# The end of a graph-and-attention kernel put in an order by hand: norms, transposes and bias adds between the products

## The chip, the cores and the metric

The kernel runs on 1 core of one Trainium2 chip. The metric is the device time of one execution in microseconds (us). A core has a matrix engine (PE; the loading of its stationary operand is listed apart as PEld), a vector engine (DVE), an activation engine (ACT), a general engine (POOL), an engine that here only issues transfers (SP), and 16 DMA engines that serve the transfers of all queues. Each engine works through its own instructions in order and waits for others by semaphores. Products are summed in PSUM; tiles lie in SBUF; HBM is the memory outside.

## The reference

A graph convolution with a residual, and then a transformer layer on 1250 nodes of width D = 1024, with 16 heads that gate 8 experts each. The change touches only the last sums and the feed forward:

```python
x = x + gnn(layernorm(x), edges, W, b)            # x1 in the kernel
src = layernorm(x)                                # z in the kernel
src2 = moe_attn(src, Wq, Wk, Wv, Wo, Wsel_v, Wsel_o)
#   ... last step of it: einsum('bhsp,bhse,hepd->bsd', o, go, Wo)
src = src + src2
src = ln(src, ln1_g, ln1_b)
src2 = relu(src @ W1 + b1) @ W2 + b2              # W1: 1024 x 512, W2: 512 x 1024
src = src + src2
out = x + ln(src, ln2_g, ln2_b)
```

`ln` subtracts the mean, divides by the root of the variance plus 1e-5, multiplies by a gain and adds a shift. All is float32.

## The kernel before

Nodes lie in NT = 10 tiles of KT = 125 rows; two tiles make a chunk of 250 columns (NQ = 5 chunks). Every float32 product is made as three products of a value's rounded part and its remainder: `dot` (L152 to L156) issues hi x hi, hi x lo, lo x hi. A weight block of 128 x 1024 is loaded by SP into `w_raw` (L127, a pool of 2), ACT rounds it into `w_hi` (L138) and DVE makes `w_lo` (L144); `move` (L147 to L150) is a transfer of 125 rows in two pieces of 112 and 13, by default on SP's queue.

**Outputs** (`outputs`). Its 16 blocks of 4 weights (`order`, `blocks`) run over the 5 chunks: 80 steps. A step (k, c) is, for i in 0, 1 (tile t = 2c + i) and for each half of the 1024 columns, a sum of 12 matmuls of 512 columns: four quarters. At its start the step loads the next block's weight number c (for c < 4) and asks for `gb`, the gates of the step after next (L928). After each quarter DVE adds the sum to `acc[t]` (L1018). After quarter (0, 0) DVE gates the next step's heads (`gated`, L949 to L951) and SP loads `oc` and `r` for the step after (L937, L943; `r` in two more pieces at chunk 4). After (0, 1) and (1, 1) ACT and DVE split what comes next into `go_hi` (L958) and `go_lo` (L960). After (1, 0) the weight loaded in this step is split. `acc`, one array in the profile, appears there under the names of the memory that it takes over: `acc`, `zT`, `gate_v`. The sums have 5 PSUM banks, the transposes 2 (`banks[:] = [5, 2]`).

**Feed forward** (`feed_forward`). For each chunk c: 4 sums over W1 of 24 matmuls of 256 columns (f in 0..3), each followed by relu on ACT (L1072), its rounding (L1073) and remainder (L1074) into `hT`; then 4 sums over W2 of 12 matmuls of 512 columns, added to `acc` (L1085). `first_norm(c)` norms the chunk's two tiles: `moments` on DVE (two L162, L164, a root on ACT L166, L168), `affine` on DVE (L178, L179), then `transposed` (L181 to L191): per half, four transposes on PE, a rounding on ACT, a remainder on DVE, into the two parts of `sT`; POOL adds `b2` to the tile (L1044). `last_norm(t)` loads `x1` (L150) from HBM, POOL adds the shift `c2` to it (L1053), and DVE does moments and affine with `x1` as the shift; SP stores the result.

**Order.** The program up to block 14 of the outputs stands under `tc.manual_schedule`: every engine, SP included, gets its instructions in the order in which the code issues them. Block 15 and the feed forward stand outside: there a planner orders each engine's instructions when the program is built. The tables of the feed forward and the first two tiles of `x1` came to stand where the attention ends, at 1978 us.

```python
    with tc.manual_schedule(engines=all_engines):
        for _ in range(4 * (NT * (2 * NP - 1) + 4) - made):
            next(main)
    next(tail)
    for _ in main:
        pass
    for _ in tail:
        pass
```

Of the kernel before, what the change touches and what calls it, by code (L numbers as in the profile page):

```python
# [11 lines left out]
F32 = mybir.dt.float32  # L12
F32R = mybir.dt.float32r
# [4 lines left out]
ALU = mybir.AluOpType  # L18
# [14 lines left out]
P = 128  # L33
# [39 lines left out]
def gnn_ffn_kernel(  # L73
# [50 lines left out]
    def loaded(block, raw=None):  # L124
        if raw is None:
            raw = raws[0].tile([P, D], F32, name="w_raw")
        nc.sync.dma_start(raw, block)  # L127
        return raw
# [47 lines left out]
    def affine(out, x, mean, rs, scale, shift):  # L176

        nc.vector.scalar_tensor_tensor(out, x, mean, scale, op0=ALU.subtract, op1=ALU.mult)  # L178
        nc.vector.scalar_tensor_tensor(out, out, rs, shift, op0=ALU.mult, op1=ALU.add)  # L179

    def transposed(targets, y, psum_tile):  # L181

        for half in range(2):
            p = psum_tile([P, 4, KT])
            for k in range(4):
                d0 = (4 * half + k) * P
                nc.tensor.transpose(p[:, k, :], y[:, d0 : d0 + P], ident[:KT, :KT])
            for hi, lo, c0, cols in targets:
                to = (slice(None), slice(4 * half, 4 * half + 4), slice(c0, c0 + cols.stop - cols.start))
                nc.scalar.copy(hi[to], p[:, :, cols])  # L190
                nc.vector.tensor_tensor(lo[to], p[:, :, cols], hi[to].bitcast(F32), ALU.subtract)  # L191
# [722 lines left out]

    acc = []

    def outputs(acc_pool, pool):

        last = QW * (NC - 1)

# [42 lines left out]
        order = [(j, half_e) for j in range(NP) for half_e in range(2)]  # L963
        blocks = {k: [wo[j, 4 * half_e + i] for i in range(4)] for k, (j, half_e) in enumerate(order)}
        steps = [(k, c) for k in range(len(order)) for c in range(NQ)]

        def acc_load(t):
            acc.append(acc_pool(t))
# [32 lines left out]
            yield  # L1001
        after = []
        for m, (k, c) in enumerate(steps):
            raw = loaded(blocks[k + 1][c]) if c < 4 and k + 1 < len(order) else None
            following = m + 1 < len(steps)
            fetch(m + 2, True)
            for i in range(2):
                t = 2 * c + i
                if k == 0 and t + 2 < NT:
                    acc_load(t + 2)  # L1010
                for half in range(2):
                    cols = slice(512 * half, 512 * half + 512)
# [5 lines left out]
                    nc.vector.tensor_tensor(acc[t][:, cols], acc[t][:, cols], p, ALU.add)  # L1018
                    if following and half:
                        parts[i] = parts_of(current, i)  # L1020
                    elif following and i == 0:
                        current = gated(found.pop(0), *held)
                        fetch(m + 2, False)
                    elif raw is not None:
                        after.append(rounded(raw))
                    yield
            if c == NQ - 1:
                w, after = after, []


    def feed_forward(ftab, work):
        b1_s = ftab.tile([P, NF], F32, name="b1_s")
        nc.sync.dma_start(b1_s, b1)
        g1, c1 = broadcast_row(ftab, ln1_g, "g1"), broadcast_row(ftab, ln1_b, "c1")
        b2_s = broadcast_row(ftab, b2, "b2_s")
        g2, c2 = broadcast_row(ftab, ln2_g, "g2"), broadcast_row(ftab, ln2_b, "c2")

        def first_norm(c):
            sT = [work.tile([P, ND, QW], F32R, name=f"sT{k}") for k in range(2)]
            for i in range(2):  # L1040
                s = acc[2 * c + i]
                affine(s, s, *moments(s, "a"), g1[:KT], c1[:KT])
                transposed([(*sT, KT * i, slice(0, KT))], s, side_bank)
                nc.gpsimd.tensor_tensor(s, s, b2_s[:KT], ALU.add)  # L1044
            for part in sT:
                nc.scalar.copy(part[:, :, 2 * KT :], part[:, :, : QW - 2 * KT].bitcast(F32))
            return sT

        def last_norm(t):
            s = acc[t]  # L1050
            x1 = work.tile([KT, D], F32, name="x1")
            move(x1, x1_d[t])
            nc.gpsimd.tensor_tensor(x1, x1, c2[:KT], ALU.add)  # L1053
            mean, rs = moments(s, "b")
            step = D if t < NT - 1 else D // 2
            for c in range(0, D, step):
                affine(s[:, c : c + step], s[:, c : c + step], mean, rs, g2[:KT, c : c + step], x1[:, c : c + step])
                move(out[KT * t : KT * (t + 1), c : c + step], s[:, c : c + step])

        sT = first_norm(0)  # L1060
        yield
        w1s = [weights(w1[k]) for k in range(4)]
        w2s = [weights(w2[k]) for k in range(4)]
        for c in range(NQ):
            hT = [work.tile([P, NF, QW], F32R, name=f"hT{k}", bufs=1) for k in range(2)]
            for f in range(NF):
                p = bank([P, QW])
                for d in range(ND):
                    w = [part[:, 512 * (d % 2) + P * f : 512 * (d % 2) + P * (f + 1)] for part in w1s[d // 2]]
                    dot(p, w, [part[:, d, :] for part in sT], d == 0, d == ND - 1)  # L1070
# [4 lines left out]
            if c + 1 < NQ:  # L1075
                sT = first_norm(c + 1)
            for i in range(2):
                s = acc[2 * c + i]
                for half in range(2):
                    cols = slice(512 * half, 512 * half + 512)  # L1080
                    p = bank([KT, 512])
                    for f in range(NF):
                        dot(p, [part[:, f, KT * i : KT * (i + 1)] for part in hT],
                            [part[:, cols] for part in w2s[f]], f == 0, f == NF - 1)
                    nc.vector.tensor_tensor(s[:, cols], s[:, cols], p, ALU.add)  # L1085
                last_norm(2 * c + i)

    f_ctx = ctx.enter_context(ExitStack())
    per_head = 4 * NT
    main, spare = [], []  # L1090

    def acc_tile(t):

# [10 lines left out]
    with tc.tile_pool(name="attp", bufs=1) as apool:  # L1104
        w = [weights(wv[0, k]) for k in range(4)]
        with tc.manual_schedule(engines=all_engines):
            heads = attention(apool)
            with tc.tile_pool(name="vpool", bufs=2) as vpool:
                for k, _ in enumerate(values(apool, vpool, w)):
                    if k >= per_head - lead:  # L1110
                        next(heads)
                    if k == H * per_head - 4 * NZ - 1:
                        z2_ctx.close()
                        ring[:0] = [ctx.enter_context(tc.tile_pool(name="ring2", bufs=3, side="right"))] * 3
                        gop = ctx.enter_context(tc.tile_pool(name="gop", bufs=1, side="right"))
                        main.append(outputs(acc_tile, gop))
                    elif main:
                        next(main[0])
            made = sum(1 for _ in zip(heads, main[0]))
# [6 lines left out]
    tail = feed_forward(ftab, work)  # L1126
# [82 lines left out]
```

## Time and profile before

| | us |
|---|---|
| median of 3 runs | 2961.8 (2959.9 to 2963.07) |
| the profiled execution | 2961.16 |
| its span, first to last instruction | 2959.4 |
| PE busy | 2849.7 (96%) |
| DVE busy | 2120.9 (72%) |
| ACT busy | 993.0 (34%) |
| POOL busy | 569.1 (19%) |

All figures below are from that one execution, and times are counted from the start of the span. A row of the timeline has the start, the duration, engine, line, operation, result and operands with their shapes, how many it merges, and in brackets how long the engine stood idle before and what released it. A row such as `x2` merges several instructions that follow each other; SP's rows are issues of transfers, not the transfers. Matmuls overlap in the pipeline, so their rows are longer than the distance between their starts. The granted clock of PE is 1.00 at full speed.

### The profile page before, as it was taken

Reading aid. Unit: us, or ns where it says so; the run is one execution under the profiler, and the core shown is the slowest. Engines: PE = TensorE matmul, PEld = TensorE weight load, DVE = VectorE, ACT = ScalarE, POOL = GpSimd, SP = SyncE. Lnnn points to the kernel's source line nnn. Section 1 sums busy time; section 2 is a strip of 40 time slices with the busy share of each in tenths; the row PEclk is TensorE's granted clock in tenths of the full one; section 3 lists DMA queues with packets and bytes.
Section 4 is the critical chain, followed back from the end, with each engine's and each line's share of the span. In section 5 each row is a group of like instructions: output and inputs, shape, how many; then the busy total and the mean of one; then the engine's idle time right before and its main releaser. Section 6 shows DMA issues by size and latency. Waiting matters only on the chain. (4 is left out here: it accounts for less than half of the span.)

```text
span 2959.4 us, 40398 instructions
## 1 busy us (share of the span) xinstructions
PE 2849.7 (96%) x14018; PEld 2349.2 (79%) x14018; DVE 2120.9 (72%) x3588; ACT 993.0 (34%) x1706; POOL 569.1 (19%) x945
## 2 busy tenths in 40 slices
PE   6989899999999999999999999899999999999998
PEld 4767699978887887788888888777777777777787
DVE  7974487647777777778778787866666666656885
ACT  5772233324343433434434344321111111111222
POOL 2000011113333333333333333310000000000113
PEclk9999899999999999999999999999999999999999
DMA  3114456644555554555555555884444444444312
GB/s 117 56 44 146 150 163 169 197 99 125 151 132 134 134 142 124 144 140 147 130 152 139 144 132 129 209 217 128 114 119 121 114 123 117 115 121 119 112 52 88
DMA packets 229320, 385.45 MB, mean 130 GB/s; under 512 B 43369, under 2 KB 176489, under 8 KB 228946
## 3 DMA queue, kind: packets, MB, share of 16 engines
q1 hardware_dynamic: 176898, 273.49, 33.3%
q0 software_dynamic: 51888, 104.18, 14.6%
q10 hardware_dynamic: 320, 5.12, 0.6%
q8 instruction: 111, 1.82, 0.3%
q14 instruction: 103, 0.84, 0.1%
HBM read 220.73 MB, written 62.16 MB: 96 GB/s over the span
## 5 line engine op out<-in xcount | busy, mean ns | idle before, releaser
L154 PE MATMUL mm<-w_hi,go_hi 128*125 128x512 f32 x1280 | 507.9, 397 | 4.5 <-DVE zT L1018 3.4
L155 PE MATMUL mm<-w_lo,zT 128*128 128x512 f32 (+1 forms) x1280 | 506.4, 396 | 4.3 <-DVE w_lo L144 3.9
L155 PE MATMUL mm<-w_lo,go_hi 128*125 128x512 f32 x1280 | 508.8, 398 | 0.0
L154 PE MATMUL mm<-w_hi,zT 128*128 128x512 f32 (+1 forms) x1280 | 506.5, 396 | 1.0 <-ACT w_hi L138 1.0
L156 PE MATMUL mm<-w_hi,go_lo 128*125 128x512 f32 x1280 | 506.7, 397 | 0.7 <-DVE go_lo L960 0.7
L156 PE MATMUL mm<-w_hi,zT 128*128 128x512 f32 (+1 forms) x1280 | 505.3, 395 | 0.0
L755 ACT CAST att_hi<-turned 128x512 fp32r<-128x512 f32 x400 | 239.5, 621 | 455.5 <-DVE turned L798 279.5
L736 POOL DMA_DIRECT2D turned<-p x640 | 342.5, 542 | 80.8 <-ACT p L725 44.3
L1018 DVE TENSOR_TENSOR zT<-zT,mm 125x512 f32<-125x512 f32 x256 | 175.5, 686 | 220.5 <-PE mm L156 216.3
L798 DVE STREAM_TRANSPOSE turned<-turned 128x1280 f32<-128x1280 f32 x160 | 232.4, 1490 | 135.7 <-DMA q<-kq_d 57.5
L958 ACT CAST go_hi<-gb 128x500 fp32r<-128x500 f32 x160 | 98.3, 615 | 660.1 <-PE mm L155 289.1
L724 DVE TENSOR_REDUCE most<-side 128x1 f32<-128x1250 f32 x160 | 231.0, 1444 | 108.2 <-PE side L721 106.7
L725 ACT ACTIVATE p<-side,most 128x1250 f32<-128x1250 f32 x160 | 209.2, 1307 | 289.4 <-DVE most L724 284.7
L154 PEld LDWEIGHTS mm<-w_hi,go_hi 128*125 128x125 f32 x1280 | 239.1, 187 | 66.0 <-DVE zT L1018 4.1
L156 PEld LDWEIGHTS mm<-w_hi,go_lo 128*125 128x125 f32 x1280 | 238.9, 187 | 61.9 <-DVE go_lo L960 1.2
L155 PEld LDWEIGHTS mm<-w_lo,go_hi 128*125 128x125 f32 x1280 | 238.7, 186 | 59.2
L156 PEld LDWEIGHTS mm<-w_hi,zT 128*128 128x128 f32 (+1 forms) x1280 | 238.0, 186 | 59.5
L155 PEld LDWEIGHTS mm<-w_lo,zT 128*128 128x128 f32 (+1 forms) x1280 | 238.4, 186 | 44.3 <-DVE w_lo L144 9.4
L154 PEld LDWEIGHTS mm<-w_hi,zT 128*128 128x128 f32 (+1 forms) x1280 | 238.3, 186 | 35.8 <-ACT w_hi L138 1.2
L760 DVE TENSOR_TENSOR att_lo<-turned,att_hi 128x512 fp32r<-128x512 f32 x400 | 262.4, 682 | 0.0
L778 PE MATMUL po<-att_hi,v 128*128 128x256 f32 (+1 forms) x800 | 215.0, 290 | 33.8 <-ACT o L785 33.5
L144 DVE TENSOR_TENSOR w_lo<-w_raw,w_hi 128x1024 fp32r<-128x1024 f32 x154 | 189.5, 1231 | 43.6 <-ACT w_hi L138 43.3
(234 smaller groups left out, 4611.3 us busy)
## 6 DMA issues: line engine op xcount, KB each, us to landing
turned<-p SPq DMA_DIRECT2D x640, 80.0 KB
turned<-p POOLq DMA_DIRECT2D x640, 80.0 KB, 3.3
gb<-g_d SPq DMA_DIRECT2D x160, 250.0 KB
w_raw<-in_wv SPq DMA_DIRECT2D x64, 512.0 KB
w_raw<-in_wo SPq DMA_DIRECT2D x64, 512.0 KB
q<-kq_d POOLq DMA_DIRECT2D x80, 256.0 KB, 4.3
oc<-o_d SPq DMA_DIRECT2D x160, 125.0 KB
kq_d<-qk_hi SPq DMA_DIRECT2D x64, 156.2 KB
```

Source lines behind the costliest of these rows:

```text
L144: (lo_engine or nc.vector).tensor_tensor(lo, raw, hi.bitcast(F32), ALU.subtract)
L154: nc.tensor.matmul(p, lhsT=lhs[0], rhs=rhs[0], start=start, stop=False)
L155: nc.tensor.matmul(p, lhsT=lhs[0], rhs=rhs[1], start=False, stop=False)
L156: nc.tensor.matmul(p, lhsT=lhs[1], rhs=rhs[0], start=False, stop=stop)
L724: nc.vector.tensor_reduce(most, side[:, :N], AX.X, ALU.max, negate=True)
L725: nc.scalar.activation(p[:, (2 * n + i) % 3, :N], side[:, :N], AF.Exp, bias=most, accum_out=inverse[h][:, 2 * c + i : 2 * c + i + 1])
L736: queue.dma_start(t[NB * a : NB * (a + 1), :, KA * b : KA * (b + 1)], both[NB * b : NB * (b + 1), :, KA * a : KA * (a + 1)])
L755: nc.scalar.copy(hi, x)
L760: nc.vector.tensor_tensor(lo, x, hi.bitcast(F32), ALU.subtract)
L778: nc.tensor.matmul(po, lhsT=v_of[h][:rows, t, :], rhs=part[:rows, :, NB * b : NB * (b + 1)], start=(first and b == 0 and part is parts[0]) ...
L798: nc.vector.transpose(turned[n][:, i], turned[n][:, i])
L1018: nc.vector.tensor_tensor(acc[t][:, cols], acc[t][:, cols], p, ALU.add)
```

## The change

Block 15 and the feed forward come under the manual order too, and a table `also` says what the outputs do after which quarter, on top of their own work. `at(k, q, ...)` enters it after quarter q (0 to 19) of block k; `end` is 15.

- Block 12: one of the five tables of 128 x 1024 is loaded after the first quarter of each step.
- Blocks 13 and 14: in each step one tile of `x1` is loaded after quarter (0, 0), DVE adds `c2` to it after (1, 0), and SP stores it to the same place in HBM. `last_norm` then loads the sum; POOL's adds are gone.
- Block 14 also loads and splits two of the W2 weights, into memory of their own; block 15 has W1 as its next block, and loads the other two of W2 at its end.
- Block 15: moments and affine of tiles 0 to 3, and the transposes of tiles 0 and 1 by halves, after quarters of their own.
- Feed forward: norms stand between the products of W1, transposes between those of W2, half by half; `b2` is added by DVE; the second norm of the odd tiles moves into the next chunk's products of W1. `sT` has one buffer instead of two.

```diff
-    def transposed(targets, y, psum_tile):
-
-        for half in range(2):
+    def transposed(targets, y, psum_tile, halves=(0, 1)):
+
+        for half in halves:
...
+        blocks[len(order)] = [w1[k] for k in range(4)]
...
-            raw = loaded(blocks[k + 1][c]) if c < 4 and k + 1 < len(order) else None
+            raw = loaded(blocks[k + 1][c]) if c < 4 else None
...
+                    for what, *args in also.pop((k, t, half), ()):
+                        what(*args)
                     yield
             if c == NQ - 1:
                 w, after = after, []
+        w1s.extend(w)
...
+        def w2_split(k):
+            parts = None
+            if k < 2:
+                parts = [ftab.tile([P, D], F32R, name=f"w2_{part}{k}") for part in ("hi", "lo")]
+                nc.scalar.copy(parts[0], w2s[k])
+            w2s[k] = rounded(w2s[k], None, parts)
+
+        def x1_load(t):
+            x1s[t] = work.tile([KT, D], F32, name="x1")
+            move(x1s[t], x1_d[t])
+
+        def x1_shift(t):
+            nc.vector.tensor_tensor(x1s[t], x1s[t], rows["c2"][:KT], ALU.add)
+            move(x1_d[t], x1s[t])
...
+        def turn(t, half):
+            c, i = divmod(t, 2)
+            if i == half == 0:
+                sTs[c] = [work.tile([P, ND, QW], F32R, name=f"sT{k}", bufs=1) for k in range(2)]
+            sT = sTs[c]
+            transposed([(*sT, KT * i, slice(0, KT))], acc[t], side_bank, (half,))
+            if half and c:
+                add_b2(t)
+            if i and half:
+                for part in sT:
+                    nc.scalar.copy(part[:, :, 2 * KT :], part[:, :, : QW - 2 * KT].bitcast(F32))
...
+        def last_affine(t, c, n):
+            cols = slice(c, c + n)
+            affine(acc[t][:, cols], acc[t][:, cols], *rss[t], rows["g2"][:KT, cols], x1s[t][:, cols])
+            move(out[KT * t : KT * (t + 1), cols], acc[t][:, cols])
+
+        def last_moments(t):
+            x1_load(t)
+            rss[t] = moments(acc[t], "b")
...
+        for q, (row, name) in enumerate(((ln2_b, "c2"), (ln1_g, "g1"), (ln1_b, "c1"), (b2, "b2"), (ln2_g, "g2"))):
+            at(end - 3, 4 * q, constant, row, name)
+        for t in range(NT):
+            k, q = divmod(4 * t, 2 * NT)
+            at(end - 2 + k, q, x1_load, t)
+            at(end - 2 + k, q + 2, x1_shift, t)
+        for k in range(2):
+            at(end - 1, 3 + 4 * k, w2_load, k)
+            at(end - 1, 5 + 4 * k, w2_split, k)
+            at(end, 15 + k, w2_load, 2 + k)
+        for t, q in enumerate((2, 5, 8, 12)):
+            at(end, q, first_moments, t)
+            at(end, q + 1, first_affine, t)
+        for k, q in enumerate((7, 10, 11, 14)):
+            at(end, q, turn, k // 2, k % 2)
         yield
...
+                t = (4, None, 5, 6, 7, 8, 9, None, None, None)[2 * c + f // 2]
+                if t is not None:
+                    (first_affine if f % 2 else first_moments)(t)
+                if c == 0 and f < 2:
+                    w2_split(2 + f)
+                elif c == 0:
+                    add_b2(f - 2)
+                if c and f == 2:
+                    last_moments(2 * c - 1)
+                if c and f == 3:
+                    last_affine(2 * c - 1, 0, D)
+            for k in range(4):
+                i, half = divmod(k, 2)
...
+                if k < 3 and c + 1 < NQ:
+                    for m in range(k, k + 1 + k // 2):
+                        turn(2 * (c + 1) + m // 2, m % 2)
+                if k == 1:
+                    last_moments(2 * c)
+                if k == 2:
+                    last_affine(2 * c, 0, D)
+        last_moments(NT - 1)
+        for c in range(0, D, D // 2):
+            last_affine(NT - 1, c, D // 2)
...
     with tc.manual_schedule(engines=all_engines):
-        for _ in range(4 * (NT * (2 * NP - 1) + 4) - made):
-            next(main)
-    next(tail)
-    for _ in main:
-        pass
-    for _ in tail:
-        pass
+        tail = feed_forward(ftab, work, also, w1s)
+        next(tail)
+        for _ in main:
+            pass
+        for _ in tail:
+            pass
```

`first_moments`, `first_affine`, `add_b2`, `w2_load` and `constant` are one call each: `moments(acc[t], "a")`, `affine` with g1 and c1, an add of `b2` on DVE, `loaded(w2[k])`, `broadcast_row`.

More of the change, by code (lines that the diff above doesn't have):

```diff
@@ L915, in gnn_ffn_kernel, with outputs @@
     acc = []
-    def outputs(acc_pool, pool):
+    def outputs(acc_pool, pool, also, w1s):
         last = QW * (NC - 1)
@@ L1028, in outputs, with feed_forward @@
                 w, after = after, []
-    def feed_forward(ftab, work):
+        w1s.extend(w)
+    def feed_forward(ftab, work, also, w1s):
         b1_s = ftab.tile([P, NF], F32, name="b1_s")
-        nc.sync.dma_start(b1_s, b1)
[L1034 to L1060, printed above, removed]
@@ new lines, in feed_forward, with constant, w2_load @@
+        rows = {}
+        w2s, x1s, sTs, rss = [None] * 4, {}, {}, {}
+        def constant(row, name):
+            rows[name] = broadcast_row(ftab, row, name)
+        def w2_load(k):
+            w2s[k] = loaded(w2[k])
+        def w2_split(k):
[7 more added lines that the diff above has]
+            move(x1s[t], x1_d[t])
@@ new lines, in x1_shift, with first_moments, first_affine @@
+        def x1_shift(t):
+            nc.vector.tensor_tensor(x1s[t], x1s[t], rows["c2"][:KT], ALU.add)
+            move(x1_d[t], x1s[t])
+        def first_moments(t):
+            rss[t] = moments(acc[t], "a")
+        def first_affine(t):
+            affine(acc[t], acc[t], *rss.pop(t), rows["g1"][:KT], rows["c1"][:KT])
+        def turn(t, half):
[9 more added lines that the diff above has]
+                    nc.scalar.copy(part[:, :, 2 * KT :], part[:, :, : QW - 2 * KT].bitcast(F32))
@@ new lines, in add_b2, with at @@
+        def add_b2(t):
+            nc.vector.tensor_tensor(acc[t], acc[t], rows["b2"][:KT], ALU.add)
+        def last_affine(t, c, n):
[5 more added lines that the diff above has]
+            rss[t] = moments(acc[t], "b")
+        def at(k, q, *what):
+            also.setdefault((k, q // 2, q % 2), []).append(what)
@@ new lines, in feed_forward @@
+        end = 2 * NP - 1
+        nc.sync.dma_start(b1_s, b1)
+        for q, (row, name) in enumerate(((ln2_b, "c2"), (ln1_g, "g1"), (ln1_b, "c1"), (b2, "b2"), (ln2_g, "g2"))):
[8 more added lines that the diff above has]
+            at(end, 15 + k, w2_load, 2 + k)
@@ L1061, in feed_forward @@
+        for t, q in enumerate((2, 5, 8, 12)):
[3 more added lines that the diff above has]
+            at(end, q, turn, k // 2, k % 2)
         yield
-        w1s = [weights(w1[k]) for k in range(4)]
-        w2s = [weights(w2[k]) for k in range(4)]
         for c in range(NQ):
@@ L1069, in feed_forward @@
                     w = [part[:, 512 * (d % 2) + P * f : 512 * (d % 2) + P * (f + 1)] for part in w1s[d // 2]]
-                    dot(p, w, [part[:, d, :] for part in sT], d == 0, d == ND - 1)
+                    dot(p, w, [part[:, d, :] for part in sTs[c]], d == 0, d == ND - 1)
                 r = work.tile([P, QW], F32, name="relu")
@@ L1074, in feed_forward @@
                 nc.vector.tensor_tensor(hT[1][:, f, :], r, hT[0][:, f, :].bitcast(F32), ALU.subtract)
-            if c + 1 < NQ:
-                sT = first_norm(c + 1)
-            for i in range(2):
-                s = acc[2 * c + i]
[L1079 to L1086, printed above, removed]
+                t = (4, None, 5, 6, 7, 8, 9, None, None, None)[2 * c + f // 2]
[11 more added lines that the diff above has]
+                i, half = divmod(k, 2)
+                s = acc[2 * c + i]
+                cols = slice(512 * half, 512 * half + 512)
+                p = bank([KT, 512])
+                for f in range(NF):
+                    dot(p, [part[:, f, KT * i : KT * (i + 1)] for part in hT],
+                        [part[:, cols] for part in w2s[f]], f == 0, f == NF - 1)
+                nc.vector.tensor_tensor(s[:, cols], s[:, cols], p, ALU.add)
+                if k < 3 and c + 1 < NQ:
[8 more added lines that the diff above has]
+            last_affine(NT - 1, c, D // 2)
     f_ctx = ctx.enter_context(ExitStack())
     per_head = 4 * NT
-    main, spare = [], []
+    main, spare, also, w1s = [], [], {}, []
     def acc_tile(t):
@@ L1115, in gnn_ffn_kernel @@
                         gop = ctx.enter_context(tc.tile_pool(name="gop", bufs=1, side="right"))
-                        main.append(outputs(acc_tile, gop))
+                        main.append(outputs(acc_tile, gop, also, w1s))
                     elif main:
                         next(main[0])
-            made = sum(1 for _ in zip(heads, main[0]))
+            for _ in zip(heads, main[0]):
+                pass
     main = main[0]
@@ L1125, in gnn_ffn_kernel @@
     work = f_ctx.enter_context(tc.tile_pool(name="fwork", bufs=2))
-    tail = feed_forward(ftab, work)
     with tc.manual_schedule(engines=all_engines):
-        for _ in range(4 * (NT * (2 * NP - 1) + 4) - made):
-            next(main)
-    next(tail)
-    for _ in main:
-        pass
-    for _ in tail:
-        pass
+        tail = feed_forward(ftab, work, also, w1s)
[3 more added lines that the diff above has]
+        for _ in tail:
+            pass
 def rotation():
```

## The prediction

> **What bounds the kernel now.** First the stretches of the end, by engine: after the two times come busy time (instructions) of PE, PEld, DVE, ACT, POOL, then granted TensorE clock, DMA share, GB/s.
>
> ```profile
> 2680.00:2740.00 60.00, 60.00 (x259) 47.73 (x258) 37.26 (x53) 10.56 (x15) 0.00 (x0) 1.00 0.44 122
> ...
> 2780.00:2800.00 20.00, 17.40 (x84) 13.77 (x82) 20.00 (x29) 5.52 (x12) 5.70 (x2) 1.00 0.24 64
> 2800.00:2820.00 20.00, 16.23 (x67) 12.47 (x68) 20.00 (x30) 4.20 (x10) 5.29 (x2) 0.86 0.00 1
> 2820.00:2840.00 20.00, 20.00 (x115) 17.59 (x114) 18.87 (x31) 5.39 (x10) 0.00 (x0) 0.89 0.17 53
> ...
> 2900.00:2920.00 20.00, 20.00 (x139) 18.35 (x139) 11.10 (x20) 5.49 (x14) 6.36 (x3) 1.00 0.34 104
> ```
>
> PE is full in the outputs and in the feed forward. It loses time only in the last output block, where DVE is 100% busy. The timeline of PE there has three waits:
>
> ```profile
> 2800.09 0.68 PE L187 MATMUL tr<-ident,zT 125*128 125x125 f32 x4 [2.69 <-DVE sT L191]
> ...
> 2813.86 0.50 PE L154 MATMUL mm<-w_hi,go_hi 128*125 128x512 f32 x1 [0.26 <-ACT go_hi L958]
> 2818.93 0.79 PE L154 MATMUL mm<-w_hi,go_hi 128*125 128x512 f32 x1 [3.42 <-DVE zT L1018]
> ```
>
> DVE is late there because norms of tiles that nobody needs yet stand before the outputs' own work, and because a DVE instruction lasts longer while POOL adds b2:
>
> ```profile
> 2794.24 3.42 DVE L179 SCALAR_TENSOR_TENSOR zT<-zT,rsa,c 125x1024 f32<-125x1024 f32 x1
> ...
> 2803.10 2.50 DVE L949 TENSOR_TENSOR oc<-oc 128x250 f32<-128x250 f32 x1
> ```
>
> L179 otherwise lasts 1.28, L949 0.41; POOL's adds run at 2793.30 (3.28) and 2802.88 (2.43).
>
> **What goes.** The waits: 2.69 + 0.26 + 3.42 = 6.4 us. After each long one matmuls start 0.43 us apart instead of 0.23, to 2803.9 and to 2824.4: 3.1 us hold 6 matmuls and 4 transposes (1.9 us at full clock), 5.5 us hold 13 matmuls (3.0), so 1.2 + 2.5 = 3.7 us. Sum 10.1. [...] Waits of up to 1.67 us (at 1945.0) left the clock at 1.00 in the trace. Further, the old schedule loads the tables and two x1 tiles in one lump at 1978 to 1992 and lets POOL add to x1 at 1997; PE then loses 0.7 us (1.26 busy of 2000 to 2002, a go_lo of 2.00 us). One table a step in block 12 waits for nothing and DVE is 62% busy: 0.7 gained. Total 10.8.
>
> **What comes, 1: x1 in blocks 13 and 14.** The largest new thing. Each of these ten steps now loads an x1 tile, adds c2 on DVE, and stores it again. SP's queue in a step of today:
>
> ```profile
> 2695.02 1.26 SPq L928 DMA_DIRECT2D gb<-g_d  x2
> 2699.23 1.23 SPq L937 DMA_DIRECT2D oc<-o_d  x2
> 2700.55 1.19 SPq L943 DMA_DIRECT2D r<-r_d  x2
> 2701.78 0.59 SPq L127 DMA_DIRECT2D w_raw<-in_wo  x1
> 2706.20 1.26 SPq L928 DMA_DIRECT2D gb<-g_d  x2
> ```
>
> A step is 11.2 us. Call 0 the step's first add (L1018 at 2696.50). oc goes out at 2.73, when gb (L951) is done; r 1.32 later; the x1 load takes the place of w_raw, at 5.28. The add of c2 stands behind the third quarter's add and w_lo: DVE comes to it at 5.6 + 0.6 + 1.1 = 7.35. The load has to land in 2.1 us. How long it takes, from SP's and POOL's rows of the feed forward:
>
> ```profile
> 2906.09 0.77 SPq L150 DMA_DIRECT2D out<-zT  x2
> 2906.96 1.35 SPq L150 DMA_DIRECT2D x<-x_d  x2
> ```
>
> ```profile
> 2912.45 2.40 POOL L1053 TENSOR_TENSOR x<-x,c 125x1024 f32<-125x1024 f32 x1 [13.21 <-DMA x<-x_d]
> ```
>
> 5.5 us behind a store of the same size; the other two such pairs give 6.0 and 6.2. In windows of 1 us the data of one transfer start some 1.25 us after the issue (w_raw: 2701.78, data from 2703), 500 KB fill 1.7 us of the engines, and the user starts 1.7 us after the last data. Alone it is thus 1.25 + 1.7/0.9 + 1.7 = 4.8 (bounds 4.4, as the store issued at 2881.92 had data after 0.85, and 6.2). So DVE stands still for 2.9 us in the first step. Behind it in DVE's queue are the last quarter's add, go_lo, and all of the next step; behind it on SP is the store, then w_raw and gb.
>
> It feeds itself. From the start of one c2 add: 1.13 + 0.6 + 0.6 (last quarter's add, go_lo, next step's add begins) + 2.73 + 1.32 + 1.23 = 7.6 to the next x1 load, + 4.8 to land = 12.4. By the transfers: 1.25 to the store's issue, 1.25 to its data, 8.2 of service a step (4.8 now, 0.43 of 11.2; a store and a load 3.4, summed over 2882 to 2891), 1.7 = 12.4 with engines full, 13.0 at 0.92. I take 12.7, 1.5 us over the step. Nine repeats: four at 1.5; two without a w_raw behind them, bound by the issues, 1.3 each; one with four r transfers instead of two (2.47 against 1.19), 2.6; the two behind w2 loads, by transfers (512 KB more, 1.6), 3.2 and 3.1. Together 6 + 2.6 + 2.6 + 6.3 = 17.5, with the first 2.9 = 20.4. What covers: go_lo of the last quarter is normally done at 9.75 and PE wants it at 13.76, so 4.0 are free. PE loses **16.3**. Bounds: 0 (landing in 3.3 or less closes the loop inside 11.2) and 23 (engines at 0.85: 13.8 a cycle). I take the middle, which both ways give. The stalls are 1.3 to 3 us each; where the clock falls PE uses time it would have waited. [...]
>
> The adds themselves, 1.2 us of DVE a step, lie in its idle 38%; that cover is gone where the wait takes it, which the loop counts.
>
> **What comes, 2: block 15 by hand.** DVE per step: four adds 0.6, gating 2.0, go_lo 2 x 0.6, w_lo 1.13 = 6.7 (starts apart). Added: four moments (0.6 + 0.6 + 0.12 and the round trip to ACT's root, 1.9), four affines 2.4, four halves of a turn 0.6, nearly all in quarters 2 to 14. Summed quarter by quarter, DVE's lag grows to 4.8 us at quarter 13; go_lo then misses PE by 0.7 us, once more by 0.3. Price **1.0** (0 to 5). Transposes wait for affines that are 3 quarters old: 0.
>
> **What comes, 3: feed forward.** Today 0 stalls. In the chunks c = 1 and 2 quarter f = 2 puts two moments (2 x 2.0) between hT of f = 2 and of f = 3, and ACT's relu of f = 3 stands behind both roots. relu then starts 2.9 us after the product, + 0.45 + 0.45 (copy) = 3.8; the first three f of the next product cover 9 x 0.231 = 2.1. Stall 1.5 to 1.7 per chunk. Where the second product's half is done, DVE has add, turn, b2 add (1.2, now its own), moments, then add, two turns, b2, affine (2.4): the last lo half of sT is ready 1.2 us after PE wants it in c = 1 and 2, 0.3 in c = 0 and 3. Sum 2 x 1.5 + 2 x 1.2 + 2 x 0.3 = **6.0** (2 to 9). Waits this short leave the clock. Taking POOL's sixteen adds off saves nothing on the path here, PE being full; they cost DVE ten b2 adds of 1.2, counted.
>
> **What comes, 4: the tail.** x1 of the last tile is today loaded at 2934; now its load stands behind the store of tile 8, which waits for its affine. With 0 the last matmul's end: add of quarter 2 at -2.6, affine 8 done at +0.5, store, load, landed 5.3 to 6.2 after the store's issue: +5.9 to 6.7. The last shift wants it at +3.8. Then two halves: done at 8.0 to 8.9, today 6.0; the last store's tail stays. **+2.2** (1 to 3).
>
> Sum against the profiled execution (2961.2 around a span of 2959.4; the median is 0.6 above): 2961.2 - 10.8 + 16.3 + 1.0 + 6.0 + 2.2 = 2975.9. Forecast **2976**.
>
> **Rivals.** (a) *The waits for x1 don't add up:* landing in some 3.3 us, the 4.0 of slack absorb what is left; term 1 is 0: 2959.6, within 0.2%. For it: w_raw's lone engine time is short; against: no row lands under 4.4. (b) *It does what it says, faster:* as (a), and DVE's queue in the feed forward clears earlier than I add it up (waits 1, tail 1, block 15 0): 2961.2 - 10.8 + 2 = 2952.4. For it: DVE is only 55% busy from 2900 to 2920. It decides if landing is under 3.3 and roots return within a quarter. (c) *The one SP queue fills:* engines at 0.85, cycle 13.8, term 1 = 23, and half clock after waits over 2.7 us adds 3: 2986. For it: in the lump of 1980 to 1998 gb, oc and x1 moved at only 190 to 230 GB/s; against: out and x1 moved at 270.
>
> **Numbers.** Forecast 0.55 (own range 2967 to 2984), (a) 0.18, (b) 0.14, (c) 0.13. A measurement of this kernel can't tell less than about 0.2%, 5.9 us. Slower 0.65 (forecast, less its lowest part, and c), same 0.20, faster 0.15. The range of 8 in 10: 2953 to 2986.
>
> **What would show it.** Right: in blocks 13 and 14 DVE idle before the c2 add on the x1 load, ten times, some 3 us each, steps of 12 to 14 us; no wait over 1 us in block 15; PE waiting on hT and sT by 1 to 2 us in c = 1 and 2; DVE waiting on x1 before the last shift. Wrong: steps of 11.2 us there (then a or b), or a clock under 1.00 through blocks 13 and 14 (c).

## The result, and the profile after

| | before | changed kernel |
|---|---|---|
| median of 6 runs, us | 2963.78 (2959.9 to 2969.11) | 2990.55 (2981.07 to 2997.66) |
| ratio, 95% interval | 1 | 1.0087 (1.0066 to 1.0107) |
| the profiled execution, us | 2961.16 | 2997.66 |
| its span, us | 2959.4 | 2995.9 |

The changed kernel is slower by 27 us. The direction was forecast; the time, 2990.55, lies above the range (2953 to 2986). The profiled execution is 36.5 us longer than that of before. Some 10 us of this are no work of the change: the attention, whose instructions are the same, ends later, and in the twelve profiles shown or used here the end of block 12 falls between 2644.3 and 2659.7. So the stages are counted from there: from the last add of block 12 (before 2649.04, after 2659.68) to the start of the first relu (first W1 sum done), to the start of the last matmul, to the end of the span. Blocks 13 and 14 are counted to the start of their last add but one, because the last one stands behind a c2 add in DVE's queue. PE's own rows, from the first matmul of block 13 to the first of block 15, say the same: 111.79 us before, 135.43 after, 23.6 more.

| us | before | after | difference |
|---|---|---|---|
| blocks 13 and 14, to their last add but one | 108.98 | 132.44 | +23.46 |
| from there to the first relu (block 15, first W1 sum) | 76.33 | 67.90 | -8.43 |
| to the last matmul | 114.16 | 123.04 | +8.88 |
| to the end | 10.89 | 12.84 | +1.95 |
| sum | 310.36 | 336.22 | +25.86 |

In the rows of the same stretches as before (times, PE, PEld, DVE, ACT, POOL, clock, DMA share, GB/s), PE is no longer full in blocks 13 and 14, which now end at 2794.7, and its clock falls there:

```profile
2680.00:2740.00 60.00, 53.87 (x222) 41.70 (x221) 32.34 (x44) 9.34 (x13) 0.00 (x0) 0.97 0.72 175
2780.00:2800.00 20.00, 16.93 (x66) 13.11 (x66) 9.79 (x13) 2.79 (x4) 0.00 (x0) 0.91 0.55 141
2800.00:2820.00 20.00, 19.85 (x86) 15.10 (x85) 16.51 (x26) 4.36 (x6) 0.00 (x0) 1.00 0.60 159
2820.00:2840.00 20.00, 18.13 (x76) 14.14 (x75) 18.87 (x29) 5.64 (x10) 0.00 (x0) 0.91 0.45 133
2900.00:2920.00 20.00, 19.37 (x136) 17.30 (x134) 18.46 (x28) 4.91 (x13) 0.00 (x0) 1.00 0.34 104
```

In the first of them, which lies in blocks 13 and 14 in both kernels, DVE does less than before (32.34 against 37.26). An engine that is late and yet idle is waiting. The page's costliest group says for whom PE waits (busy, mean ns, idle before, what ended it):

```profile
L156 PE MATMUL mm<-w_hi,go_lo 128*125 128x512 f32 x1280 | 510.7, 399 | 19.1 <-DVE go_lo L961 19.0
```

In PE's timeline these are eight waits in blocks 13 and 14 (17.1 us) and one in block 15 (1.87); two in the feed forward are for `hT`:

```profile
2689.33 0.50 PE L156 MATMUL mm<-w_hi,go_lo 128*125 128x512 f32 x1 [1.33 <-DVE go_lo L961]
2703.58 0.50 PE L156 MATMUL mm<-w_hi,go_lo 128*125 128x512 f32 x1 [2.85 <-DVE go_lo L961]
...
2758.90 0.79 PE L156 MATMUL mm<-w_hi,go_lo 128*125 128x512 f32 x1 [4.00 <-DVE go_lo L961]
...
2826.61 0.49 PE L156 MATMUL mm<-w_hi,go_lo 128*125 128x512 f32 x1 [1.87 <-DVE go_lo L961]
...
2896.59 0.50 PE L154 MATMUL mm<-w_hi,hT 128*125 128x512 f32 x1 [1.40 <-ACT hT L1125]
...
2924.30 0.50 PE L154 MATMUL mm<-w_hi,hT 128*125 128x512 f32 x1 [1.93 <-ACT hT L1125]
```

Why `go_lo` is late stands in DVE's and SP's timelines of one step. DVE:

```profile
2672.88 1.23 DVE L1061 TENSOR_TENSOR x<-x,c 125x1024 f32<-125x1024 f32 x1 [3.02 <-DMA x<-x_d]
...
2682.64 1.23 DVE L144 TENSOR_TENSOR w_lo<-w_raw,w_hi 128x1024 fp32r<-128x1024 f32 x1 [2.65 <-ACT w_hi L138]
2686.86 1.23 DVE L1061 TENSOR_TENSOR x<-x,c 125x1024 f32<-125x1024 f32 x1 [2.99 <-DMA x<-x_d]
```

SP between these two c2 adds:

```profile
2674.14 0.75 SPq L150 DMA_DIRECT2D x_d<-x  x2
2674.94 0.92 SPq L127 DMA_DIRECT2D w_raw<-in_wo  x1
2675.95 1.27 SPq L929 DMA_DIRECT2D gb<-g_d  x2
2677.94 1.23 SPq L938 DMA_DIRECT2D oc<-o_d  x2
2679.22 1.24 SPq L944 DMA_DIRECT2D r<-r_d  x2
2680.51 1.35 SPq L150 DMA_DIRECT2D x<-x_d  x2
```

DVE stands for x1 in front of the c2 add (L1061) in each of the ten steps, 2.5 to 5.5 us. The ten adds start 13.93 us apart on average, (2798.28 - 2672.88) / 9, where a step of PE takes 11.17. From one add's start, the next x1 load is issued 7.63 later, as worked out (7.6); so it is, to 7.8, in seven of the nine repeats, while in the two with four `r` transfers it is 9.80 and 10.60. But it lands 6.35 after that, behind five other transfers. Two windows, one in this step and one behind its end, show what the DMA engines do meanwhile:

```profile
2675.40:2685.20 9.80, 9.80 (x44) 7.80 (x43) 5.55 (x8) 2.19 (x3) 0.00 (x0) 1.00 0.95 227
2687.00:2688.90 1.90, 1.00 (x5) 0.46 (x3) 1.90 (x3) 0.00 (x0) 0.00 (x0) 1.00 0.00 0
```

They are full for 9.8 us (share 0.95), then quite empty (0.00), since the next store waits for DVE's add.

At the end the last shift of the last tile waits for an x1 that was asked for behind the store of tile 8 (SP, then DVE):

```profile
2984.82 1.36 SPq L150 DMA_DIRECT2D x<-x_d  x2
```

```profile
2990.18 0.75 DVE L179 SCALAR_TENSOR_TENSOR gate_v<-gate_v,rsb,x 125x512 f32<-125x512 f32 x1 [3.04 <-DMA x<-x_d]
```

### The profile page after: what moved, and what is told of

The parts are those of the page before. It is cut to its first block, busy times and chain, and to the rows that moved or that the text cites. A ratio compares the mean times of both kernels' runs of the same rounds, so it can differ in the third digit from the quotient of the medians.

```text
span 2995.9 us, 40397 instructions
## 1 busy us (share of the span) xinstructions
PE 2862.3 (96%) x14018; PEld 2354.0 (79%) x14018; DVE 2137.0 (71%) x3608; ACT 992.8 (33%) x1706; POOL 520.7 (17%) x925
## 4 chain that ended last, share of the span: by engine, by line
PE 48%; DVE 15%; DMA 13%; SPq 6%; issue 5%; ACT 3%; POOL 3%; DVEq 0%; ACTq 0%; POOLq 0%
PE mm L155 13%; PE mm L156 13%; PE mm L154 13%; DMA turned<-p 6%; SPq L736 5%; DVE turned L798 4%; PE mm L494 3%; POOL turned L736 3%; DVE most L724 2%; DVE att_lo L760 2%; PE po L778 2%; DMA x<-x_d 2%; PE side L721 2%; DMA q<-kq_d 1%; ACT w_hi L138 1%
```

## The experiments

The theory is that the time goes into a loop: DVE stands in its queue before a c2 add, what is behind it comes late, and so does the next x1 load. The stages from the end of block 12 are compared, in us, with the same ends as above; "ratio" is to runs of the kernel before on the same chip.

| kernel | blocks 13, 14 | to first relu | to last matmul | to the end | sum | ratio (95%) |
|---|---|---|---|---|---|---|
| before | 108.98 | 76.33 | 114.16 | 10.89 | 310.36 | |
| changed kernel | 132.44 | 67.90 | 123.04 | 12.84 | 336.22 | 1.0087 (1.0066 to 1.0107) |
| early loads | 108.97 | 63.50 | 123.00 | 13.00 | 308.47 | 0.9987 (0.9976 to 0.9998) |
| c2 in the feed forward | 108.97 | 63.46 | 128.69 | 18.60 | 319.72 | 1.0022 (1.0008 to 1.0036) |
| no store | 125.04 | 64.92 | 123.05 | 13.84 | 326.85 | no interval |
| lead of three quarters | 118.43 | 62.77 | 123.01 | 13.17 | 317.38 | no interval |
| c2 on GpSimd | 145.28 | 72.11 | 123.01 | 13.04 | 353.44 | no interval |
| early, roots, last x1 | 108.97 | 63.47 | 117.82 | 10.23 | 300.49 | 0.9964 (0.9951 to 0.9977) |
| the same, b2 on GpSimd | 108.97 | 64.08 | 115.80 | 10.58 | 299.43 | 0.9951 (0.9932 to 0.9971); again: 0.996 (0.994 to 0.998) |
| the order by hand alone | 108.98 | 64.10 | 124.26 | 15.37 | 312.71 | 1.0002 (0.999 to 1.0014) |
| before, biases on DVE | 108.98 | 71.67 | 114.13 | 10.84 | 305.62 | 0.9992 (0.9979 to 1.0004) |

### Early loads

```diff
         for t in range(NT):
-            k, q = divmod(4 * t, 2 * NT)
-            at(end - 2 + k, q, x1_load, t)
+            k, q = divmod(4 * t + 2 * NT - 3, 2 * NT)
+            at(end - 3 + k, q, x1_load, t)
+            k, q = divmod(4 * t, 2 * NT)
             at(end - 2 + k, q + 2, x1_shift, t)
```

> The changed kernel with the x1 load of each step in blocks 13 and 14 issued five quarters before its c2 add instead of two; load, add and store are all kept, so bytes and DVE work are the same. Theory (a loop: DVE stands before the c2 add until the load lands, gb and go_lo of the next step come late, so does the next load): the load lands in 5 to 8 us, five quarters are 14, so DVE's waits on x vanish, steps return to 11.2 us, PE's 17.1 us of go_lo waits in these blocks fall below 2 and the clock stays at 1.00; 20 to 23 us less, the median at 2967 to 2971 beside 2963.8 of the kernel before. Rival 1 (the transfers themselves fill SP's queue, whoever waits): gb and oc land late instead, and more than 8 us of the go_lo waits stay; less than 12 us gained. Rival 2 (DVE has too much to do with the c2 adds): its waits go but PE's stay near 17; no gain.

PE's waits in blocks 13 and 14 are gone, all of them, with the same bytes and the same DVE work. The ten c2 adds in DVE's timeline start without a wait, 11.05 us apart on average (9.15 to 12.45; the first two are shown), and the stretch that showed PE at 53.87 of 60 is full:

```profile
2665.93 1.22 DVE L1061 TENSOR_TENSOR x<-x,c 125x1024 f32<-125x1024 f32 x1
2677.10 1.22 DVE L1061 TENSOR_TENSOR x<-x,c 125x1024 f32<-125x1024 f32 x1
```

```profile
2680.00:2740.00 60.00, 60.00 (x259) 47.81 (x259) 44.05 (x60) 11.71 (x16) 0.00 (x0) 1.00 0.83 217
```

The engines move 217 GB/s here, against 175 in the changed kernel: bandwidth was not short, it was unused while everyone waited. Rival 1 and rival 2 fall. The gain up to the first relu is 200.34 - 172.47 = 27.9 us, more than the 20 to 23 expected: besides the 23.5 in blocks 13 and 14, the wait of 1.87 in block 15 and the slow matmuls after it are gone too (4.4), so these had been carried over from the loop. The ratio falls by one per cent, about 30 us.

### c2 added in the feed forward

```diff
-        def x1_shift(t):
-            nc.vector.tensor_tensor(x1s[t], x1s[t], rows["c2"][:KT], ALU.add)
-            move(x1_d[t], x1s[t])
...
             cols = slice(c, c + n)
+            nc.vector.tensor_tensor(x1s[t][:, cols], x1s[t][:, cols], rows["c2"][:KT, cols], ALU.add)
             affine(acc[t][:, cols], acc[t][:, cols], *rss[t], rows["g2"][:KT, cols], x1s[t][:, cols])
...
-            at(end - 2 + k, q, x1_load, t)
-            at(end - 2 + k, q + 2, x1_shift, t)
```

> The changed kernel without any x1 load, c2 add and store in blocks 13 and 14; c2 is added by DVE in the feed forward, just before the last affine of each tile (ten adds of 1.2 us move there). Loop theory and rival 1: blocks 13 and 14 lose nothing, some 22 us less there, and the feed forward gets 0 to 6 us dearer (in the chunks c = 1 and 2 DVE's queue gets 1.2 us longer ahead of the last lo half of sT or hT of f = 3; the tail 1.2): 16 to 22 us less in all, the median at 2969 to 2975. Against the kernel with the early loads it is 0 to 6 us slower under the loop theory (the early loads cost nothing there), and at least 8 us faster under rival 1.

Up to the first relu it equals the early loads to 0.05 us, so they cost nothing there. Against the changed kernel it gains 16.5 us by the stages, as expected. But beside the early loads it loses 11.3, not 0 to 6: 5.7 in the feed forward, where PE's waits grow from 4.6 to 8.8 us (three on `hT`: 2.53, 3.06, 1.10), and 5.6 in the tail, where two x1 waits of 2.33 and 3.60 and three adds stand in a row. In this order DVE has no time for it there, and bringing the c2 adds forward is worth these 11.3 us. Roots ahead of the relu and a late x1 of the last tile have a part in them; no run adds c2 on DVE in the feed forward without these two.

### Without the store

```diff
             nc.vector.tensor_tensor(x1s[t], x1s[t], rows["c2"][:KT], ALU.add)
-            move(x1_d[t], x1s[t])
```

> The changed kernel without the store of x1 after its c2 add in blocks 13 and 14 (the outputs lack c2 by this); loads at their late place, adds kept. If the cycle of 14.0 us goes by the transfers in SP's queue (store, w_raw, gb, oc, r, x1 load, one after another at a rate of some 0.84), it loses the store's 1.7/0.84 = 2.0 us and is bound by the issues instead, some 12.4 us; later loads then land 4.5 to 5 us after their issue instead of 6.4, and PE's waits in these blocks fall from 17 to 5 to 9 us. If the landing is slow for another reason (the path of a load by itself), it stays at 6.4 and the cycle at 13.5 or more, with over 13 us of waits.

The adds are 13.05 us apart instead of 13.93; the loads land after 5.18 us on average (4.61 to 5.98) instead of 5.63 (4.14 to 7.60); PE's waits in these blocks are 10.8 us. This lies between the two expectations. In the nine repeats two contain four `r` transfers instead of two and take 14.87 and 14.32; the other seven average 12.61, near the 12.4 of a cycle bound by the issues. The edit takes away more than a transfer: SP no longer stands for the c2 add, so `w_raw` goes out 4.1 us ahead of it (2673.02, add at 2677.14) in place of 2.1 behind it. Both together are worth 0.9 us of the 2.8 by which the cycle exceeds the step, and most of the loop stands without it: 7.6 to the issue and some 5 to land are 12.6 already.

### A lead of three quarters

The edit is that of the early loads with `2 * NT - 1` in place of `2 * NT - 3`.

> The changed kernel with each x1 load of blocks 13 and 14 issued one quarter earlier: three quarters before its c2 add instead of two, which on SP is just ahead of oc and r instead of behind them. Loop theory: from the start of a c2 add SP needs 1.26 us to the store, 0.8 to w_raw, 1.0 to gb, and 2.0 to what follows gb, so the x1 load goes out 5.1 us after it instead of 7.63; with the 4.8 to 6.4 us of landing the cycle is 9.9 to 11.5, against a step of 11.17: the loop no longer feeds itself. DVE waits on x for 0 to 1.6 us at a time, PE's go_lo waits in blocks 13 and 14 sum to under 3 us, and these blocks lose 0 to 4 us against the kernel with the early loads instead of 23.5. Rival (the landing is long because the queue always holds much, a queue of 8 to 10 us): each step gains just the 2.8 us of one quarter until the store and w_raw catch up, and 8 to 15 us of loss stay.

DVE waits for x1 only twice (1.14 and 0.68), as the loop theory says, and yet 9.5 us are lost in blocks 13 and 14 (8.7 up to the first relu), as the rival says. The reason is neither's: the loop closes through another load. SP now issues the x1 load ahead of `w_raw`, and `w_lo` stands ahead of the c2 add in DVE's queue. First SP, then ACT, then DVE:

```profile
2666.47 0.76 SPq L150 DMA_DIRECT2D x_d<-x  x2
2667.28 1.40 SPq L150 DMA_DIRECT2D x<-x_d  x2
2668.72 0.35 SPq L127 DMA_DIRECT2D w_raw<-in_wo  x1
```

```profile
2676.60 1.05 ACT L138 CAST w_hi<-w_raw 128x1024 fp32r<-128x1024 f32 x1 [4.07 <-DMA w_raw<-in_wo]
```

```profile
2677.68 1.22 DVE L144 TENSOR_TENSOR w_lo<-w_raw,w_hi 128x1024 fp32r<-128x1024 f32 x1 [2.33 <-ACT w_hi L138]
2678.82 1.22 DVE L1061 TENSOR_TENSOR x<-x,c 125x1024 f32<-125x1024 f32 x1
```

From the add at 2665.23: 1.24 to the store, 0.81 to the x1 load, 1.44 to `w_raw`, 7.88 until ACT has it, 2.22 to the next add: 13.59. With the lead of five quarters `w_raw` is issued right behind the store and ACT has it after 6.90: 1.25 + 0.79 + 6.90 + 2.23 = 11.17, the step itself. There ACT's copy is done 0.05 us before DVE comes to `w_lo` (2675.92, 2675.97), and in four later steps DVE waits for it, 0.20 to 0.98 us. So that kernel has little to spare either.

### c2 on GpSimd

```diff
-            nc.vector.tensor_tensor(x1s[t], x1s[t], rows["c2"][:KT], ALU.add)
+            nc.gpsimd.tensor_tensor(x1s[t], x1s[t], rows["c2"][:KT], ALU.add)
             move(x1_d[t], x1s[t])
```

> The changed kernel with the ten c2 adds of blocks 13 and 14 on GpSimd instead of DVE; loads at their late place, so that now GpSimd stands and waits for x1, and DVE's queue holds no instruction that waits for it. Theory A (what costs time is the standing of DVE, behind which go_lo and the gating queue): DVE's idle time before go_lo goes, PE's waits in blocks 13 and 14 fall below 3 us; DVE instructions beside GpSimd's adds last 1 to 2 us longer, inside DVE's idle time. Theory B (any queue that stands in line closes the loop): SP stands before the store until GpSimd's add of 2.4 to 3.3 us is done, and w_raw, gb, oc, r and the next x1 load stand behind it; the cycle becomes 6.4 (store to the next load) + 4.8 to 6.4 (landing) + 2.5 to 3.4 (add) = 13.7 to 16.2 against a step of 11.17, and with some 3 to 4 us of slack for gb and oc and 4 for go_lo PE loses 10 to 30 us in these blocks, now with DVE waiting on oc, r or gb. I take B for the likelier.

Theory B: with DVE free of the wait, the loss is larger, 36.3 us in blocks 13 and 14 (10 to 30 expected) and 8.6 more up to the first relu than with early loads. SP stands in its place, before the store (SP, then GpSimd, then SP, then DVE):

```profile
2665.48 2.96 SPq L150 DMA_DIRECT2D x<-x_d  x2
```

```profile
2673.12 3.39 POOL L1061 TENSOR_TENSOR x<-x,c 125x1024 f32<-125x1024 f32 x1 [13.46 <-DMA x<-x_d]
```

```profile
2676.54 0.75 SPq L150 DMA_DIRECT2D x_d<-x  x2
2677.34 0.92 SPq L127 DMA_DIRECT2D w_raw<-in_wo  x1
```

```profile
2686.24 1.23 DVE L144 TENSOR_TENSOR w_lo<-w_raw,w_hi 128x1024 fp32r<-128x1024 f32 x1 [8.59 <-ACT w_hi L138]
```

GpSimd's adds start 15.8 us apart, (2799.40 - 2657.25) / 9, inside the 13.7 to 16.2 expected. What I had not seen is that DVE waits for `w_raw` (8.59 here), not for `oc`. ACT waits for it too (10.13 before `w_hi` at 2685.16), and behind `w_hi` in its queue stands the `go_hi` for which PE waits 3.50 us at 2686.77.

### Roots behind the relu, the last x1 early

The early loads, and two edits in the feed forward. `stats` is the DVE part of `moments`, `root` the rest of it; odd tiles of the second norm likewise:

```diff
-                if t is not None:
-                    (first_affine if f % 2 else first_moments)(t)
+                if t is not None and f % 2:
+                    rss[t] = root(mvs.pop(t), "a")
+                    first_affine(t)
+                elif t is not None:
+                    mvs[t] = stats(acc[t], "a")
...
         def last_moments(t):
-            x1_load(t)
+            if t < NT - 1:
+                x1_load(t)
+            if t == NT - 2:
+                x1_load(NT - 1)
```

> The kernel with the early x1 loads, and two edits in the feed forward: the roots of the moments go to ACT (and reciprocal to DVE) in quarter f = 3 behind that quarter's relu and copy, while their statistics stay at f = 2; and the last tile's x1 is loaded together with tile 8's, ahead of the store of tile 8. Theory: PE's waits on hT (1.40 and 1.93 us) vanish, because ACT's relu of f = 3 no longer stands behind the roots; the 3.0 us wait on x before the last affine vanishes, and the tail from the last matmul to the end falls from 12.4 to 10.5. Together 5 us less than with the early loads alone, a median of 2962 to 2966. Rival for hT: the statistics on DVE (four bn_stats, 0.6 us each) hold hT's lo part whatever ACT does; then 1 us or more stays in each of the two chunks. Rival for the tail: the end is set by the last two stores and not by x1; then the tail stays above 12.

Both stages fall, by 5.2 and 2.8 us; 5 had been expected in all, and both rivals fall. The `hT` waits are gone: in the changed kernel ACT's relu of f = 3 (2895.64) had stood directly behind the second root (2895.44). Two waits on `sT` are left in the feed forward:

```profile
2873.28 0.39 PE L154 MATMUL mm<-sT,w_hi 128*128 128x256 f32 x1 [0.48 <-ACT sT L1097]
...
2898.47 0.39 PE L154 MATMUL mm<-sT,w_hi 128*128 128x256 f32 x1 [0.49 <-ACT sT L1097]
```

### b2 on GpSimd again

In `add_b2`, `nc.gpsimd` for `nc.vector`, on top of the last kernel. The second expectation belongs to the repeat.

> The kernel with early loads, roots behind the relu and the early x1 of the last tile, and with the ten adds of b2 back on GpSimd (in the feed forward; c2 stays on DVE). In the kernel before one such add on GpSimd (2.4 to 3.3 us) made the DVE instruction beside it 1.1 to 2.1 us longer, which is about what the add costs on DVE itself (1.2). Theory: it is a wash for DVE's load, but the product's add behind it waits longer for its tile; from the first W1 sum to the last matmul 117.8 becomes 117 to 121, the median within 4 us of the kernel without this edit. Rival (moving the biases to DVE is what costs in the feed forward): the sT waits of 0.5 us go and the stage falls by 1 us or more.

> The kernel with early loads, roots behind the relu, the early x1 of the last tile and b2 on GpSimd once more, to narrow its ratio (0.9951, 0.9932 to 0.9971 so far). By the stages of its profile (299.4 us from the end of block 12 on, against 310.4 in the kernel before, and 1.0 less at the block of tables and x1 loads at the beginning of the outputs) it should be 12 us under the kernel before: 0.9960. A ratio above 0.9975 would say that the stages don't tell the time.

The rival holds: from the first relu to the last matmul 2.0 us less, and no wait of PE is left there. (0.6 come back in block 15, where GpSimd's first two adds now run, at 2796.87 and 2809.00.) In this order b2 on DVE, which makes it busy 55.94 of 60 us between 2860 and 2920, costs more than GpSimd's interference (three DVE instructions longer by 2.4 us in all). The repeat gives the expected 0.996. By its stages this is the fastest of the kernels, 0.4 to 0.5% under the kernel before; the 1.1 us to the one ahead of it are too few for the ratios to show.

### The order by hand alone

x1 is loaded in the feed forward ahead of its use, c2 and b2 are added by GpSimd, roots stand behind the relu; blocks 13 and 14 have no x1.

```diff
             move(x1s[t], x1_d[t])
+            nc.gpsimd.tensor_tensor(x1s[t], x1s[t], rows["c2"][:KT], ALU.add)
...
+                if k % 2 == 0:
+                    x1_load(2 * c + k // 2)
```

> The changed kernel keeping only its order by hand: no x1 traffic in blocks 13 and 14 (no load, c2 add or store there), in the feed forward x1 of a tile loaded four products ahead of its affine and c2 added on GpSimd right behind the load, b2 on GpSimd too, roots of the moments behind the relu of f = 3. Theory (the order by hand gains 13 us up to the first W1 sum, and the transfers of x1 in blocks 13 and 14 buy nothing that GpSimd didn't do beside the products): 108.97 us for blocks 13 and 14, 172.4 to 173.1 up to the first W1 sum, 115.5 to 118 from there to the last matmul, 10 to 11 after it: 298 to 302 us in all beside 310.4 in the kernel before and 299.4 with early loads and b2 on GpSimd; ratio to the kernel before 0.994 to 0.998. Rival (the transfers in the feed forward or GpSimd's twenty adds, which stretch DVE instructions beside them by 1.1 to 2.1 us, cost what the change moved them away for): 3 us or more on top, waits on sT, hT or x in the feed forward.

The first half is as expected (173.08), the rest is the rival's: 8.5 us more than with early loads and b2 on GpSimd up to the last matmul, and 4.8 in the tail. On SP pairs of x1 loads go out just after a store that waits for its affine, and GpSimd's adds stretch the affine beside them to 3.4 us (1.28 alone):

```profile
2873.84 3.42 DVE L196 SCALAR_TENSOR_TENSOR zT<-zT,rsb,x 125x1024 f32<-125x1024 f32 x1 [2.29 <-POOL x L1076]
```

This is one placement of these loads, with the adds on GpSimd. It doesn't show that none is good in the feed forward; beside this one the forward c2 adds with early loads are 13.3 us better.

### Before, with the biases on DVE

`nc.vector` for `nc.gpsimd` in the two bias adds of the kernel before, nothing else.

> The kernel before with one part of the change alone: the adds of b2 and of c2 on DVE instead of GpSimd, everything else and the planner's order as before. In its last output block four adds on GpSimd stretch the DVE instructions beside them by 1.1, 2.1, 2.1 and 1.5 us, 6.8 in all; on DVE they would take 4 x 1.15 = 4.6. If the order by hand is what brings the 10.7 us there, this edit alone brings only 0 to 4 of them, and PE's waits of 2.69 and 3.42 us stay over 1 us each; the feed forward, with DVE busy 55%, stays within 2 us. Rival (the engine of the biases is what brings the gain): both long waits vanish and the stage from block 13 to the first W1 sum falls by 8 us or more. The median within 4 us of before, or 8 below it.

4.7 us less up to the first relu, slightly more than expected. Three waits remain, in PE's timeline:

```profile
2806.54 0.65 PE L187 MATMUL tr<-ident,zT 125*128 125x125 f32 x4 [1.23 <-DVE sT L191]
2808.41 0.71 PE L187 MATMUL tr<-ident,zT 125*128 125x125 f32 x4 [1.22 <-DVE sT L191]
2810.09 0.79 PE L156 MATMUL mm<-w_hi,go_lo 128*125 128x512 f32 x1 [0.98 <-DVE go_lo L960]
```

So of the 10.8 us that the order by hand gains up to the first relu (185.31 to 172.47, less 2.0 for transposes that merely move), the engine of the b2 adds alone brings 4.7 in the old order. By the median no difference is shown, and the trace has the reason: the edit loses 3.9 us elsewhere. From an add ahead of the lump of tables and x1 at the start of the outputs to the end of block 12 it takes 686.53 us in place of 682.65. In the lump DVE, not GpSimd, now stands for x1, and PE behind it (DVE, then PE):

```profile
2000.34 1.23 DVE L1053 TENSOR_TENSOR x<-x,c 125x1024 f32<-125x1024 f32 x1 [7.03 <-DMA x<-x_d]
```

```profile
2006.02 0.50 PE L154 MATMUL mm<-w_hi,go_hi 128*125 128x512 f32 x1 [2.84 <-ACT go_hi L958]
```

## Why the prediction was wrong, and where it was right

**What goes: right.** With the loop taken out, the stage up to the first relu is 12.8 us shorter than before. 16 transposes of it merely moved into the feed forward (1.02 us for eight, 2.0 in all). 10.8 are gained; 10.1 were summed. The lump of tables and x1 at the start of the outputs was put at 0.7: from an add ahead of it to the end of block 12 it takes 681.66 us in place of 682.65, 1.0 less.

**Term 1, x1 in blocks 13 and 14: the mechanism right, the size wrong, and here the prediction failed.** It said 16.3; it is 23.5. The first landing (4.81 against 4.8), the first wait (3.02; 2.9 was written, where 5.28 + 4.8 - 7.35 makes 2.7) and, in seven of nine repeats, the way from one add to the next load (7.6) hold, and the 4.0 us of slack fit: 3.0 + 9 x (13.93 - 11.17) - 4.0 = 23.8. What failed is the step "+ 4.8 to land = 12.4 ... I take 12.7". The 4.8 is the landing of a load with little ahead of it. In the loop it has the store, `w_raw`, `gb`, `oc` and `r` ahead, issued in the 6.4 us before it, and lands after 5.9 to 7.6 in five of the nine repeats (4.1 to 5.0 in the four where no `w_raw` stands ahead or SP comes to it later). So the four repeats that were put at 1.5 us over the step each lie 2.4 to 3.4 over it, 11.6 together in place of 6.0; all nine make 24.9 in place of 17.5. The bound by transfers had been worked out too, but with 8.2 us of engine time a step at up to full speed; in the step shown the engines take 9.8 us, 0.95 busy, at 227 GB/s. With 9.8 for the 8.2 its own sum, 1.25 + 1.25 + 9.8 + 1.7, makes 14.0, and that step took 13.97. The two steps without a `w_raw` behind the store, put at 12.5, took 12.09 and 12.59. The 12.7 was the middle of two sums, and even the larger, 13.0, was too small.

**Rival (c) was the nearer one,** with a cycle of 13.8 and 23 for the term; it was given 0.13. What was held against it, out and x1 moving at 270 GB/s in the feed forward, was a pair of transfers alone and not this mix of six; why the mix is slower no run shows. Its 3 us for the clock are half right. In blocks 13 and 14, by this sum, the slow clock costs hardly anything of its own: PE waits for 17.1 us there and loses some 6.4 to slow matmuls, and the two together are what DVE's cycle gives (23.8 against 23.5), as the forecast said. It costs in block 15, where nothing was left to wait for.

**Rival (a)** is what the same code does with the loads three quarters earlier: 0.9987 of before, that is 2957.4 on the scale of the 2961.2 (2954 to 2961), against its 2959.6. Its reason was another, a landing in some 3.3 us; no load that DVE waited for landed in less than 4.1.

**Term 2, block 15 by hand:** 1.0 predicted, 4.4 seen, with a wait of 1.87 us where none over 1 had been expected. With early loads it is 0, so the 4.4 are the loop's: its lag comes into a block where DVE has no time to catch up.

**Term 3, feed forward:** 6.0 predicted; 8.9 less 2.0 for the moved transposes is 6.8. The `hT` waits are 1.40 and 1.93 (1.5 each predicted) and have the cause given, shown by the kernel that moves the roots. The `sT` waits are smaller (0.55 twice; 1.2 twice predicted). The other 2.2 us are no waits in the trace; 1.6 of them went with the `hT` waits. What they are is open.

**Term 4, the tail:** 2.2 predicted, 1.95 seen; loading the last x1 early takes off 2.8.

By these terms the change is -10.8 - 1.0 + 23.5 + 4.4 + 6.8 + 1.95 = +24.9; the prediction had +14.7. Of the 10.2 between them 10.6 come from the loop and its lag. The ratio of 1.0087 makes +25.8.

The nine loads of the loop landed 4.1 to 7.6 us after their issue, and issuing them three quarters earlier brought 27.9 us up to the first relu.

## What to carry to other kernels

Ask of every new load how long before its use it is issued, counted with everything that has been put on the same queue since the last one, and what stands behind the instruction that waits. If the wait delays the next issue, add up the way once around, on each engine and each queue that it passes: where it is longer than the step (here 13.93 us against 11.17) the loss is repeated in every step, and a resource with capacity to spare looks full and empty by turns (here the DMA engines, share 0.95 for 9.8 us and later 0.00 for 1.9). Take the cover from the loads that were there before as well: `w_raw` became the late one as soon as x1 no longer was.

## What the runs showed of the hardware

**The clock did not fall by the length of a wait alone.** In the changed kernel it stayed up after 2.16 us (at 2743.49, next starts 0.23 apart; granted 1.00 from 2743.5 to 2747.0) and fell after 1.87 us (at 2826.61, 0.43 apart from the third matmul on; granted 0.61 from 2826.6 to 2831.0); with the lead of three quarters it fell after 2.10 (at 2742.22, starts 0.43 apart from the second matmul on). After 2.85 (at 2703.58) it fell with the third matmul (granted 0.68 from 2703.6 to 2709.0). What decides between waits of nearly the same length no run shows.

**Some DVE instructions that started beside a GpSimd add ended only after it; others kept their time.** In the kernel before, GpSimd's add ends at 2793.30 + 3.28 = 2796.58, and the affine that started at 2794.24 ends at 2797.66, 1.08 later, where alone it takes 1.28. In block 15 of that kernel four adds make four DVE instructions longer, by 1.07, 2.14, 2.08 and 1.53 us, 6.8 in all. With b2 on GpSimd again, ten adds make three longer, by 0.60, 0.89 and 0.90, 2.4 in all. All seven read two tiles of SBUF and end 0.29 to 1.08 us after the add. Most of what else runs beside the ten adds sums a product or takes a remainder of `sT`, with one input in PSUM, or is a `bn_stats`, and these keep their 0.67 to 0.69 us (`bn_stats` 1.28 for two). An add of c2 or b2 to a whole tile takes 1.21 to 1.23 us on DVE in the kernels that have it there. This fits that moving the adds to DVE gained 4.7 us in one order and lost 2.0 in another, though no run changes only what stands beside them.
